# A second Strassen level in three of seven query products, keys and values with held weights, transfers placed anew

## The chip, the core and the metric

The kernel runs on one core of one Trainium2 chip. The metric is device time in microseconds, from launch to the last store: 1040.75 us as the median of three runs (1040.5 to 1040.83). Five queues work beside each other and are synchronised by semaphores: TensorE (PE, whose weight loads the profile shows apart as PEld), VectorE (DVE), ScalarE (ACT), GpSimd (POOL) and SyncE (SP), which here only issues transfers. Each of them works through its instructions in the order in which the program gives them.

## The reference, cut to what matters

Sixty-four batches of 128 tokens with 512 features go through a multi-query attention layer with 16 heads of 64 features; keys and values are shared by the heads.

```python
x = (64, 128, 512);  g_in (512,);  Wq (512, 1024);  Wkv (512, 128);  Wo (1024, 512)
xn  = layernorm(x, g_in)
q   = (xn @ Wq).reshape(b, n, 16, 64).transpose(0, 2, 1, 3) * 64**-0.5
k, v = split(xn @ Wkv)                       # 64 features each
k, v = concat([null_kv[0], k]), concat([null_kv[1], v])
sim = einsum('bhid,bjd->bhij', q, k) + concat([null_bias, attn_bias])
sim = causal and padding mask (sim);  attn = softmax(sim)
out = layernorm(einsum('bhij,bjd->bhid', attn, v).reshape(b, n, 1024) @ Wo, g_out)
return x + out
```

Everything is 32-bit float. The kernel subtracts the null key from every key and the null value from every value, and adds the null value back behind the softmax, so that the null column becomes a constant.

## The kernel before, in words

The batches are worked through in pairs. `cycle(c)` (line 935) writes out by hand one period in which four stages of four different pairs stand side by side: the query product of a pair two cycles ahead, the softmax of the pair (b0, b1), the output projection of the pair before (p, p+1), and the output layernorm of the pair before that (r, r+1). Each cycle ends with `region` (line 914), in which PE does the scores of the next pair and the attention-times-values of the present one in many small matmuls. Cycles run for c = 1 to 29 (line 1226); a prologue fills the pipe and a tail written out by hand empties it. There is no planner: the order of the calls in `cycle` is the order in each queue.

A group is four batches (512 tokens). The **query product** of a group has 4 feature pairs f; for each, `product` (line 480) and `q_one` (line 852) do one level of Strassen's scheme in Winograd's form: the two 256-token halves, the two halves of the 512 input features and the two halves of the 1024 output features are the blocks, and seven products of half size take the place of eight. Product k is two k-steps of a 128x128 weight block against 256 tokens; each such fp32 matmul appears in the trace as two weight loads and two matmuls. The sums that the scheme needs of the tokens are made on POOL (`token_sum`, line 466, four instructions per group, before issued at the end of every odd cycle), those of the weights once at the start. The results are put together from PSUM by ACT copies (`keep`, line 505; `q_out`, line 509) and DVE additions into `qT`. Two of the four feature pairs of a group are done in one cycle (h = 0 and 1), so a group takes an even and an odd cycle. The tile `a` in PSUM is used in turn by products 1, 6, 7 and 4, with a copy by ACT between each two.

**Keys and values** are made by `kv_mm` (line 353): for each batch, the tokens are the held (loaded) operand and the 128 columns of `wkv` stream. `kv_out` (line 369) subtracts the null row. The keys are then turned by DVE in 32x32 blocks and sent through DRAM to become `kT` (`keys_send`, `keys_fetch`, lines 396 and 409, five transfers per group); the values go through DRAM into four copies `vr` (`values_send`, `values_fetch`, five transfers).

The **softmax** of a batch is, per half: scores added on DVE, maximum on DVE, eight exponentials on ACT (`exps`), a reciprocal on DVE (`rinv`), a scaling on POOL (`scale`, line 618), then a block transpose on DVE (`blocks_T`, line 632), after which POOL fills the freed buffer with the bias of a batch two further on (`bias_add`, line 531). The **output projection** (`out_product`, line 743) is Strassen's scheme too; its sums (`out_sum`, line 729) are POOL's.

Of the kernel before, what the change touches and what calls it, by code (L numbers as in the profile page):

```python
# [17 lines left out]
def kernel(  # L18
# [134 lines left out]
    nkv = const.tile([P, KVN], FP, name="nkv")  # L153
# [31 lines left out]
    def load_second():  # L185
        for m in range(XB + 1, 2 * GB):
            load_x(m)
        nc.sync.dma_start(
            out=nkv, in_=cond[0:2].rearrange("r d -> (r d)").partition_broadcast(P)
# [163 lines left out]
    def kv_mm(m, pkv=None):  # L353
        g, t = divmod(m, GB)
        if pkv is None:
            pkv = ps_w.tile([P, KVN], FP, tag="w", name=f"pkv_{m}")
        for kc in range(KC):
            nc.tensor.matmul(  # L358
                pkv,
                xT[g][:, t, kc, :],  # L360
                wkv[:, kc, :],
                start=(kc == 0),
                stop=(kc == KC - 1),
            )
        return pkv

    kvts, kvds = {}, {}

    def kv_out(m, pkv):
        g, t = divmod(m, GB)  # L370
        if t == 0:
            kvts[g] = hp.tile([P, 2, GB, DH], FP, tag="kv", name=f"kvt_{g}", bufs=1)
        nc.vector.tensor_tensor(
            kvts[g][:, :, t, :],
            pkv.rearrange("p (r d) -> p r d", r=2),
            nkv.rearrange("p (r d) -> p r d", r=2),
# [3 lines left out]
    vds, kds = {}, {}  # L380

    def values_send(g):

        vds[g] = dp.tile([P, GB * DH], FP, tag="vd", name=f"vd_{g}")
        nc.sync.dma_start(out=vds[g], in_=kvts[g][:, 1].rearrange("p t d -> p (t d)"))

    def values_fetch(g):
        vr[g] = hp.tile([P, NQ, GB, DH], FP, tag="vr", name=f"vr_{g}")
        src = vds.pop(g).rearrange("(j p) e -> p j e", p=Q)
        for s in range(NQ):  # L390
            nc.sync.dma_start(
                out=vr[g][s * Q : (s + 1) * Q].rearrange("p j t d -> p j (t d)"),
                in_=src,
            )

    def keys_send(g):

        kb = hp.tile([P, 2, GB, Q], FP, tag="kb", name=f"kb_{g}", bufs=1)
        nc.vector.transpose(
            kb,  # L400
            kvts[g][:, 0].rearrange("p t (c k) -> p c t k", k=Q),
        )
        kds[g] = dp.tile([P, 2, GB * Q], FP, tag="kd", name=f"kd_{g}")
        nc.sync.dma_start(
            out=kds[g].rearrange("p c e -> p (c e)"),
            in_=kb.rearrange("p c t q -> p (c t q)"),
        )

    def keys_fetch(g):
        kT[g] = hp.tile([P, NQ, GB, Q], FP, tag="kT", name=f"kT_{g}")  # L410
# [998 lines left out]
```

## Time and profile before

| | |
|---|---|
| runs, median of 3 | 1040.75 us |
| the profiled execution | 1040.6 us; its span 1038.8 us, with 1.8 us around it |
| granted TensorE clock | 0.998 |
| busy, share of the span | PE 99%, PEld 86%, DVE 74%, POOL 68%, ACT 64% |
| idle of POOL until ACT's last attention result, line 741 | 113.0 us in 28 waits |
| one cycle in the middle | 31.45 us |

The times are those of one execution. A matmul's duration in the trace runs over into that of the next, because matmuls are pipelined: what one costs is the distance from its start to the next one's start. In a timeline row the first number is the start in microseconds from the start of the span, the second the stretch that the merged instructions take, "x8" their count, and a bracket tells for how long the engine had been idle and which instruction ended that.

### The profile page before, as it was taken

What the parts mean: (1) busy time and instruction counts of PE and PEld (TensorE: products, weight loads), DVE (VectorE), ACT (ScalarE), POOL (GpSimd) and SP (SyncE); (2) the same over time, 40 slices, a digit from 0 to 9 for tenths busy, and PEclk for the clock granted to TensorE, in tenths of its full rate; (3) what the DMA queues carried; (4) which work ended last, traced back from release to release, by engine and by line L of the source; (5) the groups of instructions that cost most, each with busy time, mean ns of one, the idle gap of its engine ahead of it and who ended that gap; (6) DMA issues with size and microseconds to landing.
All of it is one profiled execution on the core that took longest, in us unless ns stands there. A gap on an engine that the chain in (4) does not pass through costs nothing.

```text
span 1038.8 us, 31012 instructions
## 1 busy us (share of the span) xinstructions
PE 1024.2 (99%) x11856; PEld 896.4 (86%) x11856; DVE 771.2 (74%) x1664; ACT 665.9 (64%) x2799; POOL 711.0 (68%) x530
## 2 busy tenths in 40 slices
PE   8999999999999999999999999999999999999996
PEld 7888888888888888888888888888888888888875
DVE  7776677787677786677776777776786876766688
ACT  2665677565776566776656776657765657765581
POOL 3697767676775857767577676757758587666774
PEclk9999999999999999999999999999999999999999
DMA  6633160432515134151341504334151341502202
GB/s 210 157 121 85 52 182 27 146 92 94 144 52 153 57 120 128 42 169 50 127 112 67 169 25 150 88 103 137 51 154 55 123 125 42 166 12 73 83 11 92
DMA packets 68690, 105.10 MB, mean 101 GB/s; under 512 B 8641, under 2 KB 32833, under 8 KB 66753
## 3 DMA queue, kind: packets, MB, share of 16 engines
q1 hardware_dynamic: 67440, 102.08, 32.3%
q8 instruction: 96, 1.57, 0.7%
q10 hardware_dynamic: 1104, 1.05, 0.3%
q14 instruction: 50, 0.40, 0.1%
HBM read 67.45 MB, written 35.65 MB: 99 GB/s over the span
## 4 chain that ended last, share of the span: by engine, by line
PE 92%; ACT 3%; DVE 3%; DMA 1%; POOL 1%; issue 1%; POOLq 0%; DVEq 0%; ACTq 0%
PE pa L496 20%; PE pyX L758 19%; PE pc L496 10%; PE pyY L758 9%; PE ps L551 9%; PE pkv L358 5%; PE pyw L758 5%; PE pw L496 5%; PE poX L668 4%; PE pq L445 2%; ACT s L599 2%; PE pos L668 2%; PE poY L668 1%; DMA x<-in_x_dram 1%; DVE y_end L821 1%
## 5 line engine op out<-in xcount | busy, mean ns | idle before, releaser
L599 ACT ACTIVATE s<-s,nmax 128x65 f32<-128x65 f32 (+1 forms) x1024 | 377.5, 393 | 0.0
L535 POOL TENSOR_TENSOR s<-biasp,mneg 128x1552 f32<-128x1552 f32 x64 | 206.2, 3223 | 70.6 <-DVE sb L635 58.9
L599 ACT ACTIVATION_READ_ACCUMULATOR s<-s,nmax 128x1 f32 x1024 | 221.3, 216 | 0.0
L620 POOL TENSOR_TENSOR s<-s,rinv 128x1024 f32<-128x1024 f32 (+1 forms) x128 | 190.4, 1488 | 44.5 <-DVE rinv L616 44.5
L635 DVE STREAM_TRANSPOSE sb<-s 128x1536 f32<-128x1536 f32 x64 | 113.5, 1773 | 43.2 <-POOL s L620 43.0
L585 DVE TENSOR_TENSOR s<-ps,s 128x256 f32<-128x256 f32 (+2 forms) x224 | 120.0, 605 | 16.9 <-PE ps L551 14.7
L496 PE MATMUL pa<-xS,wq 128*128 128x256 f32 x480 | 123.4, 379 | 0.5 <-ACT ku L507 0.5
L758 PE MATMUL pyX<-wo,oT 128*128 128x256 f32 x512 | 121.6, 380 | 0.3 <-POOL oT L741 0.3
L741 POOL TENSOR_TENSOR yS<-oT 128x512 f32<-128x512 f32 x32 | 40.9, 1278 | 117.2 <-ACT oT L708 113.0
L708 ACT ACTIVATE oT<-poX,nv 128x256 f32<-128x256 f32 x59 | 28.0, 475 | 143.8 <-PE poX L668 74.4
L590 DVE TENSOR_REDUCE nmax<-s 128x8 f32<-128x520 f32 (+1 forms) x128 | 116.4, 948 | 0.0
L758 PE MATMUL pyX<-wT,oT 128*128 128x256 f32 x488 | 115.4, 379 | 0.3 <-POOL oT L741 0.3
L758 PEld LDWEIGHTS pyX<-wo,oT 128*128 128x128 f32 x512 | 96.8, 190 | 15.3 <-issue 1.3
L758 PEld LDWEIGHTS pyX<-wT,oT 128*128 128x128 f32 x488 | 92.6, 190 | 13.3 <-POOL oT L741 0.7
L496 PEld LDWEIGHTS pa<-xS,wq 128*128 128x128 f32 x480 | 88.9, 190 | 11.7 <-ACT ku L507 0.9
L551 PEld LDWEIGHTS ps<-kT,qT 64*64 64x64 f32 x4096 | 85.6, 134 | 11.5 <-issue 11.4
L551 PE MATMUL ps<-kT,qT 64*64 64x128 f32 (+1 forms) x4096 | 93.7, 245 | 0.6 <-issue 0.6
L517 DVE TENSOR_TENSOR qT<-pc,ku 128x256 f32<-128x256 f32 x120 | 50.4, 420 | 58.6 <-ACT ku L507 43.5
L514 ACT COPY qT<-pa 128x256 f32<-128x256 f32 x60 | 23.0, 383 | 101.7 <-PE pa L496 101.7
L288 POOL TENSOR_TENSOR rstd<-rstd,nhalf 128x1 f32<-128x1 f32 x64 | 35.7, 559 | 66.6 <-DVE rstd L287 66.6
L668 PE MATMUL pos<-sb,vr 32*64 32x128 f32 (+1 forms) x1792 | 81.0, 321 | 0.0
L668 PE MATMUL poY<-sb,vr 32*64 32x128 f32 x720 | 74.4, 347 | 0.0
(113 smaller groups left out, 2299.8 us busy)
## 6 DMA issues: line engine op xcount, KB each, us to landing
x<-in_x_dram SPq DMA_DIRECT2D x64, 256.0 KB, 5.4
res<-in_x_dram SPq DMA_DIRECT2D x64, 256.0 KB, 3.1
out_dram<-y SPq DMA_DIRECT2D x58, 256.0 KB, 2.0
xd<-xb SPq DMA_DIRECT2D x14, 1024.0 KB
xT<-xd SPq DMA_DIRECT2D x56, 256.0 KB, 6.1
vr<-vd SPq DMA_DIRECT2D x64, 128.0 KB, 8.5
kT<-kd SPq DMA_DIRECT2D x64, 64.0 KB, 9.6
kd<-kb SPq DMA_DIRECT2D x16, 128.0 KB
```

Source lines behind the costliest of these rows:

```text
L358: nc.tensor.matmul(pkv, xT[g][:, t, kc, :], wkv[:, kc, :], start=(kc == 0), stop=(kc == KC - 1),)
L496: nc.tensor.matmul(prod[tag], w[:, kc, f * P : (f + 1) * P], t[:, :, kc, :], start=(start and kc == 0), stop=(kc == HK - 1), skip_group_ch ...
L517: nc.vector.tensor_tensor(o, p, k, ALU.add)
L535: nc.gpsimd.tensor_tensor(S[b], biasp, mneg[:, t].unsqueeze(1).broadcast_to([P, R8, ROW]), ALU.add,)
L551: nc.tensor.matmul(to[r][i * DH : (i + 1) * DH, f, :], qT[g][rows, f, t, NQ - 1 - i if hf else i], kT[g][rows, 0 : NQ if hf else NQ // 2, ...
L585: nc.vector.tensor_tensor(sv, ps, sv, ALU.add)
L590: nc.vector.tensor_reduce(nmax[b][:, hf], S[b][:, :, WITH_NULL[hf]], AX.X, ALU.max, negate=True)
L599: nc.scalar.activation(row, row, AF.Exp, bias=nmax[b][:, hf, k : k + 1], accum_out=rsum[b][:, hf, k : k + 1],)
L620: nc.gpsimd.tensor_tensor(sv, sv, rinvs.pop((b, hf)).unsqueeze(2).broadcast_to([P, R8, sv.shape[2]]), ALU.mult,)
L635: nc.vector.transpose(sb.rearrange("p j e q -> p e j q"), S[b][:, :, 1 : ROW - 1].rearrange("p e (j k) -> p e j k", k=Q),)
L668: nc.tensor.matmul(po[s][rows, half], vr[g][quad(s), j, t, :], sb[quad(s), slots, r * NF : (r + 1) * NF, :], start=start, stop=True, skip_ ...
L758: nc.tensor.matmul(prod[key], h[:, c, :], w[:, c, :], start=(start and c == 0), stop=(c == HC - 1), skip_group_check=not start,)
```

## The change

Parts that go together:

- In cycles from c = 2 on (`LEAF = 2`), products 2, 4 and 3 of two feature pairs are taken together (`leaf`). Their 2x2 blocks of 128x128 are multiplied by a second level of the scheme: seven products of 128 output features by 128 input features by 128 tokens in place of eight. They come in four stages that add up in one PSUM tile of three blocks; after each stage DVE adds what is complete onto `qT`.
- What the stages need: sums of tokens on POOL (`leaf_sums`, 12 instructions of 128 columns in every even cycle), sums of weights on POOL once (`leaf_weights`, nine ahead of cycle 1's other work and three at its end), in tiles `wL` and `xL`.
- For c >= 2, products 1, 6 and 7 are copied by ACT straight into `qT` (`first_into`), product 5 is added there by DVE (in `q_one` k = 7 and the new k = 8), and the last copy of the chain (k = 4) goes.
- `qT` becomes four tiles of a quarter group each, in one copy instead of two.
- `kv_mm` holds `wkv` and streams two batches; its result is already the transposed key (partitions 0 to 63) and value (64 to 127). The keys are copied to the other partitions by one transfer; the values are turned by DVE and take two transfers out and one back.
- The calls in `cycle` stand in another order: among others `token_sum` at the top of the even cycle, `load_x`, `store` and the fetches apart from each other, the DVE maxima of b1 ahead of those of b0. The alignment of PE's instructions (`addr_align`) stands at another place with other offsets.

The core of the diff (the prologue's calls follow from it; `q_first`, `stats_part` and `gain_copy` are defined but not called):

```diff
-    def kv_mm(m, pkv=None):
+    def kv_mm(m):
...
+        pkv = ps_w.tile([P, 2 * N], FP, tag="w", name=f"pkv_{m}")
         for kc in range(KC):
             nc.tensor.matmul(
                 pkv,
-                xT[g][:, t, kc, :],
                 wkv[:, kc, :],
+                xT[g][:, t : t + 2, kc, :],
...
+        nc.vector.tensor_scalar(
+            kT[g][:, :, t : t + 2, :],
+            pkv.rearrange("p (t i q) -> p i t q", t=2, q=Q),
+            nkv, None, ALU.subtract,
+        )
...
     def values_send(g):
+        vt = hp.tile([P, NQ, GB, Q], FP, tag="vt", name=f"vt_{g}", bufs=1)
+        nc.vector.transpose(vt[DH:], kT[g][DH:])
...
+    def keys_send(g):
+        nc.sync.dma_start(out=kT[g][DH:], in_=kT[g][:DH])
...
+    def leaf_sums(g, k):
+        n = 4 if k == 3 else 3
+        xL[g, k] = gp.tile([P, n, N], FP, tag=f"xL{k}", name=f"xL{k}_{g}", bufs=1)
...
+        for o, p, m in ((t1, b12, b11), (t3, b22, b12), (t2, b22, t1), (t4, b21, t2)):
+            nc.gpsimd.tensor_tensor(o, p, m, ALU.subtract)
...
+    def leaf(c, k, stage):
...
+            leaves[k] = ps_w.tile([P, 3, N], FP, tag="w", name=f"pl{k}_{g}_{f}")
+        pw, pY, pX = (leaves[k][:, i] for i in range(3))
...
+        def mm(to, w, t, start=False):
+            nc.tensor.matmul(to, w, t, start=start, stop=True, skip_group_check=True)
+        def onto(o, p):
+            nc.vector.tensor_tensor(o, p, o, ALU.add)
...
+        if stage == 0:
+            mm(pX, w11, b11, True)
+            onto(out[:, 0, 0], one(pX))
+        elif stage == 1:
+            mm(pw, w12, b21)
+            mm(pX, v2, t2)
+            mm(pY, v1, t1)
+            onto(out[:, 0], two(leaves[k][:, 0:3:2]))
+            onto(out[:, 1, 1], one(pY))
+        elif stage == 2:
+            mm(pX, w21, t3)
+            mm(pY, v4, b22)
+            onto(out[:, :, 1], two(leaves[k][:, 1:3]))
+        else:
+            mm(pX, w22, t4)
+            onto(out[:, 1, 0], one(pX))
...
         if k == 1:
             product(g, f, 1, ps_q, "a")
-            keep("a", "p1")
+            if c >= LEAF:
+                first_into(g, f, 0)
+            else:
+                keep("a", "p1")
...
+        elif k == 8:
+            o = q_part(g, f, 1)
+            nc.vector.tensor_tensor(o, by_block("c"), o, ALU.add)
```

The order of PE's calls in a cycle from c = 2 on (qk,h is product k of feature pair h; lk.s is stage s of product k's second level): q1,0, l2.0, q5,0, q6,0, out 1, q7,0, out 2, q1,1, l2.1, key_values, q6,1, l2.2, l3.0, out 6, l2.3, q5,1, l3.1, out 5, l4.0, q7,1, out 7, l4.1, out 4, l3.2, l4.2, out 3, l4.3, l3.3, region. POOL's in an even cycle: four token_sum, leaf_sums 2, out_sum 0, pow, leaf_sums 3, out_sum 1, pow, leaf_sums 4, scale(b0,0), pow, out_sum 3, pow, scale(b0,1), out_sum 2, scale(b1,0), scale(b1,1), two bias_add. In ACT's queue the copy of q1,0 stands behind four of the eight `values_out` of the pair.

468 lines of the change are left out of this document (304 added, 164 removed).

## The prediction

> **What bounds the kernel now.** I read the page first (busy times, then the chain of work that ended last), then stretches of single cycles, then PE's timeline inside one.
>
> ```profile
> span 1038.8 us, 31012 instructions
> PE 1024.2 (99%) x11856; PEld 896.4 (86%) x11856; DVE 771.2 (74%) x1664; ACT 665.9 (64%) x2799; POOL 711.0 (68%) x530
> ...
> PE 92%; ACT 3%; DVE 3%; DMA 1%; POOL 1%; issue 1%; POOLq 0%; DVEq 0%; ACTq 0%
> ...
> 473.18:504.63 31.45, 31.45 (x369) 27.69 (x368) 23.09 (x51) 21.01 (x88) 24.28 (x19) 1.00 0.12 44
> 504.63:536.08 31.45, 31.45 (x369) 27.70 (x368) 23.87 (x54) 21.00 (x88) 19.39 (x15) 1.00 0.55 163
> ```
>
> PE holds 92% of the chain. The last two rows are an even and an odd cycle, from one region's start to the next; after the stretch stand the busy times of PE, PEld, DVE, ACT and POOL, then the granted clock. PE is busy in all of both, at full clock, so a cycle is as long as what PE is given to do. DVE has 7.6 to 8.4 us to spare, ACT 10.4, POOL 7.2 (even) and 12.1 (odd). DMA is far from full. So the change is worth what it takes from PE, less what PE must newly wait for.
>
> **What PE's work costs.** The price of a matmul is the distance from its start to the next start:
>
> ```profile
> 464.39 1.03 PE L496 MATMUL pa<-xS,wS 128*128 128x256 f32 x4
> 465.26 1.05 PE L358 MATMUL pkv<-wkv,xT 128*128 128x128 f32 x8
> 466.15 1.03 PE L496 MATMUL pa<-xS,wq 128*128 128x256 f32 x4
> 467.01 1.05 PE L358 MATMUL pkv<-wkv,xT 128*128 128x128 f32 x8
> 467.90 1.89 PE L758 MATMUL pyY<-wo,oT 128*128 128x256 f32 x8
> 469.63 1.03 PE L496 MATMUL pc<-xT,wS 128*128 128x256 f32 x4
> ...
> 465.04 1.08 PEld L358 LDWEIGHTS pkv<-wkv,xT 128*128 128x128 f32 x8
> ```
>
> Eight matmuls of 256 columns take 469.63 - 467.90 = 1.73 us; eight of 128 take 0.89 us (466.15 - 465.26, and again 467.90 - 467.01), hardly more than half, although each has its own weight load. The group behind is not late either.
>
> Second level: a product of two feature pairs was 8 matmul instructions of 256 columns (2 pairs x 2 k-steps x 2 instructions), 1.73 us. It becomes 7 blocks x 2 = 14 of 128 columns, 14/8 x 0.89 = 1.56 us. Three products a cycle, cycles 2 to 29: 3 x 28 x 0.17 = **14.5 us less** (0.1725 before rounding). Keys and values: 16 of 128 columns per pair of batches (1.78 us) become 8 of 256 (1.73 us): 0.05 x 32 pairs = **1.6 us less**. PE alone would bring 1040.6 to 1024.5.
>
> [...]
>
> **What the other queues get.**
>
> ```profile
> L517 DVE TENSOR_TENSOR qT<-pc,ku 128x256 f32<-128x256 f32 x120 | 50.4, 420 | 58.6 <-ACT ku L507 43.5 <-PE pc L496 13.2
> L373 DVE TENSOR_TENSOR kvt<-pkv,nkv 128x128 f32<-128x128 f32 x64 | 18.0, 282 | 3.5 <-PE pkv L358 3.4
> L399 DVE STREAM_TRANSPOSE kb<-kvt 128x256 f32<-128x256 f32 x16 | 6.5, 408 | 0.0
> L330 DVE STREAM_TRANSPOSE xb<-x 128x512 f32<-128x512 f32 x56 | 35.9, 680 | 0.0
> L514 ACT COPY qT<-pa 128x256 f32<-128x256 f32 x60 | 23.0, 383 | 101.7 <-PE pa L496 101.7
> ```
>
> DVE, per cycle: 6 additions at 0.42, 2 key-value subtractions at 0.28 and half a 0.41 transpose go (3.3 us). There come 4 additions for products 5 (1.7), per second-level product 3 of 128 columns and 2 of 256 (0.84 + 0.84, three times 5.1), one subtraction at 0.42, half a transpose at 0.68. That is 7.5, net +4.2 us: 23.1 to 23.9 becomes about 27.3 to 28.1 of a 30.9 us cycle. It fits, with some 3 us left for waiting. ACT loses two copies (0.77 us).
>
> In-order waits are the danger: a stage adds into a PSUM block that DVE must have read after the stage before. Between the stages of one product PE has 1.7 to 6.2 us of other work (out 3 alone between l4.2 and l4.3; out 4 and l3.2, 2.2 us, between l4.1 and l4.2). The tightest is the latter: DVE takes l4.1 only behind `blocks_T(b1)` and the projection's addition. Laying the new order out with the old durations, DVE is done with it about when PE comes to l4.2. I take nothing for it; the upper side is in the range.
>
> A wait that I do count is before q6,0, which overwrites `a` once ACT has copied q1,0 out:
>
> ```profile
> 478.47 1.13 PE L496 MATMUL pa<-xT,wq 128*128 128x256 f32 x4
> 479.44 1.03 PE L496 MATMUL pw<-xT,wq 128*128 128x256 f32 x4
> 480.31 1.03 PE L496 MATMUL pc<-xS,wS 128*128 128x256 f32 x4
> ...
> 478.62 0.47 ACT L708 ACTIVATE oT<-poX,nv 128x256 f32<-128x256 f32 x1 [4.96 <-PE pos L668]
> ...
> 480.06 0.39 ACT L507 COPY kp<-pa 128x256 f32<-128x256 f32 x1
> ...
> 968.92 0.36 ACT L507 COPY ku<-pa 128x256 f32<-128x256 f32 x1
> ...
> 969.33 1.13 PE L496 MATMUL pa<-xS,wq 128*128 128x256 f32 x4 [0.51 <-ACT ku L507]
> 970.30 1.89 PE L758 MATMUL pyY<-wo,oT 128*128 128x256 f32 x8
> ```
>
> Before, products 2 and 5 stand between them; now l2.0 (2 instructions, 0.22) and product 5 (0.87). q6,0 would start at 479.44 + 0.22 + 0.87 = 480.53. ACT's copy stands behind four `values_out` as before and ends at 480.45. The last rows show what such a release costs: copy end 969.28, start 969.33, and the four matmuls take 0.97 instead of 0.86. So 480.45 + 0.05 + 0.11 = 480.61, 0.08 us late: 28 x 0.08 = **2.2 us more**. What is queued behind it on PE is out 1, for which nobody is in a hurry.
>
> POOL gets 12 instructions of 128 columns in each of 14 even cycles, a width that it does not have now:
>
> ```profile
> L478 POOL TENSOR_TENSOR xS<-xT 128x512 f32<-128x512 f32 x30 | 38.4, 1280 | 0.0
> L727 POOL TENSOR_TENSOR wT<-wo 128x1024 f32<-128x1024 f32 x1 | 2.4, 2371 | 0.0
> L802 POOL TENSOR_TENSOR rstdo<-rstdo,nhalf 128x1 f32<-128x1 f32 x64 | 36.6, 574 | 21.8 <-DVE rstdo L798 21.8
> masks.py:199 POOL TENSOR_SCALAR_AFFINE_SELECT ident<-ident 128x128 f32<-128x128 f32 x1 | 0.3, 294 | 0.1
> ...
> 479.27 1.27 POOL L478 TENSOR_TENSOR xS<-xT,xS 128x512 f32<-128x512 f32 x1
> 482.00 1.27 POOL L741 TENSOR_TENSOR yS<-oT 128x512 f32<-128x512 f32 x1 [1.45 <-ACT oT L708]
> ...
> 489.43 1.92 POOL L620 TENSOR_TENSOR s<-s,rinv 128x1024 f32<-128x1024 f32 x1
> ...
> 73.62 1.47 POOL L741 TENSOR_TENSOR yS<-oT 128x512 f32<-128x512 f32 x1
> 75.17 1.27 POOL L741 TENSOR_TENSOR oT<-yS,oT 128x512 f32<-128x512 f32 x1
> ```
>
> From below the price is 0.29 us (affine select, one input), from above 1.28 (four times the columns). The line through 512 and 1024 columns gives 0.46 at 128 and 0.73 at 256; I take it, as the same operation. The first four, 1.8 us, fall into the idle 1.45 us behind the token sums. The other eight delay `scale(b0,1)`: from 482.00, 3.5 us into the cycle, POOL has two out_sum, two pow, scale, pow, out_sum, pow, scale = 8.7 us by the starts of the old rows, and 8 x 0.46 = 3.7, so it ends 15.9 us into the cycle. By my layout DVE comes to `blocks_T(b0)` at the same point. I take nothing for it. Once, ahead of cycle 1, come nine weight sums, 9 x 0.73 = 6.6 us, at a place where POOL does not idle (73.62 follows the output weights' sums without a gap), so cycles 1 and 2 are late by what their slack doesn't hold. Between 0 and 8.8 us (all twelve) I take **2 us more**.
>
> Transfers and SP: ten for keys and values in two cycles become four; none was on the path.
>
> ```profile
> vr<-vd SPq DMA_DIRECT2D x64, 128.0 KB, 8.5
> kT<-kd SPq DMA_DIRECT2D x64, 64.0 KB, 9.6
> ```
>
> They are needed a cycle after they are sent. `values_send` and `keys_send` now wait on SP for DVE's turning at the even cycle's end; behind them stand the residual loads and the next x load, which are used 7 us or more later. I cost this at nothing. If that cover went, an x load would delay `norm_stats` on DVE.
>
> The sum: 1040.6 - 14.5 - 1.6 + 2.2 + 2 = 1028.7. That is against the profiled execution (span 1038.8, 1.8 around it); the median is 0.15 above it, so **1029 us**.
>
> **Instruction supply.** PE's stalls without a releaser ("issue") are another unknown:
>
> ```profile
> PEld ps L551 <- issue: 11.4, 33, 0.7
> PEld pa L496 <- issue: 11.2, 29, 0.4
> ```
>
> There is one at the region's start and one behind it in each cycle; on PE each costs about 0.1 us (478.47: 0.97 to the next start instead of 0.86). PE gets 378 matmul instructions per cycle in place of 368, and the alignment moves. Both pauses gone would give 28 x 0.2 = 5.6 us more gain, one more as long as PEld's (0.35) would cost 9.8. I take no change.
>
> **The rivals.** First: the new waits are more than I count. For it: DVE at nine tenths, in order, with about twelve more points per cycle at which PE waits for it. Against it: most of them have 2 us of other work between. At 0.3 us more per cycle, 28 x 0.3 = 8.4: **1037 us**. Chance 0.17.
>
> Second, slower than before: POOL. Place: the eight `leaf_sums` ahead of the scalings of b0. The layout holds up to 0.46 us each; from there a further 0.1 makes each even cycle 0.8 us late, since `blocks_T(b0)` holds DVE, which holds l3.1 and all behind it: 14 x 0.8 = 11 us. It eats the whole gain of 11.9 us from 0.57 on, which is the price of the 128x1 power in the rows above. At 0.64, half the 512-column price, 0.18 x 8 x 14 = 20 us: **1049 us**. For it: a fixed cost per POOL instruction, as that power shows. Against it: affine select at 0.29. Chance 0.10.
>
> Third: the weight loads bind. In the key-value run the eight loads start (1.08 - 0.19)/7 = 0.127 us apart while the matmuls start 0.111 apart, so the loads lose their lead. At 0.127, 14 cost 1.78 us, 0.05 more than 8 wide ones: 84 x 0.05 = 4.2 more, 1.6 less, 4.2 of waits: **1047 us**. Against it: the longest run of narrow ones now is eight (l3.2 with l4.2), the same length as the run that shows no loss. [...] Chance 0.05.
>
> **How the numbers follow.** The forecast, 1024 to 1034, has 0.66; the rivals 0.17, 0.10 and 0.05; 0.02 is for something else. A difference under 0.2% (2 us) can't be told from no change. Faster: the forecast and four fifths of the first rival, 0.80; same 0.05; slower 0.15. The range goes from 1022 (PE's full gain and half of the pauses) to 1043 (the first rival and POOL at its break-even), which leaves out the worse part of the second rival and the third.
>
> **What would show it.** Right: a cycle of about 31.0 us, matmuls of the second level 0.111 us apart, DVE busy 27 to 28 us of it, a wait of PE on ACT at q6,0. POOL's 128-column row near 0.46. Wrong: PE idle before stages of `leaf` released by DVE (first rival), POOL's row over 0.55 with `blocks_T` waiting for `scale` (second), narrow matmuls 0.12 apart or more (third).

## The result, and the profile after

The changed kernel takes **1166.8 us** (median of 4 runs, 1161.6 to 1171.3) against 1040.8 for the kernel before on the same chip: 1.121 times as long, 95% interval 1.116 to 1.126. The forecast was 1029. The profiled execution spans 1167.0 us, 2.1 less than its own time.

In the rows, `x` are the token loads (`load_x`), `xd` the turned tokens on their way out to DRAM (`tokens_out`), `xT` the same tokens fetched back (`tokens_in`), `res` the residual rows (`load_res`) and `m` the mask; `pl` is the PSUM tile of a second-level product, `pkv` that of keys and values, `pos` one of attention times values. First the page, then one even and one odd cycle, from region to region (columns as in the prediction), then the waits: engine and tile, what it waited for, us in all, times, the longest.

```profile
span 1167.0 us, 31412 instructions
PE 1055.9 (90%) x12104; PEld 914.4 (78%) x12104; DVE 902.6 (77%) x1996; ACT 645.7 (55%) x2743; POOL 787.8 (68%) x710
```

```profile
464.52:495.76 31.24, 31.24 (x379) 27.77 (x378) 26.49 (x63) 20.20 (x86) 27.60 (x29) 1.00 0.07 27
495.76:536.72 40.96, 33.79 (x379) 28.84 (x379) 30.14 (x66) 20.30 (x86) 19.40 (x15) 0.96 0.47 131
```

```profile
DVE st L283 <- DMA x<-in_x_dram: 69.6, 19, 6.1
...
PE pl L554 <- DVE qT L557: 40.9, 21, 2.6
...
PE pkv L357 <- DMA xT<-xd: 33.7, 12, 5.0
```

The even cycle is 0.2 us shorter than before, as a gain of the second level should look, and PE fills it. The odd one is 9.5 longer, and PE stands idle in 7 us of it. Over cycles 6 to 27 the means are 31.5 and 31.5 before, 31.3 and 40.8 after. So the loss is made in odd cycles, in which tokens are fetched and a mask is made. The three waits are new (before, DVE waited 0.8 us for x in all), and this is one odd cycle: what SP issues, then where PE and DVE stop, with the idle time in brackets.

```profile
497.04 1.30 SPq L386 DMA_DIRECT2D vd<-vt  x2
498.43 1.34 SPq L392 DMA_DIRECT2D kT<-kT  x1
499.82 1.07 SPq L137 DMA_DIRECT2D res<-in_x_dram  x2
500.93 0.59 SPq L127 DMA_DIRECT2D x<-in_x_dram  x1
501.69 2.69 SPq L347 DMA_DIRECT2D xT<-xd  x4
504.48 0.59 SPq L127 DMA_DIRECT2D x<-in_x_dram  x1
505.12 0.47 SPq L144 DMA_DIRECT2D m<-in_mask_BxS_bk_dram  x1
505.69 0.54 SPq L396 DMA_DIRECT2D vr<-vd  x1
```

```profile
500.73 0.32 PE L771 MATMUL pos<-sb,vr 32*64 32x128 f32 x1 [1.64 <-issue]
...
515.17 2.83 PE L357 MATMUL pkv<-xT,wkv 128*128 128x256 f32 x8 [3.00 <-DMA xT<-xd]
517.80 1.89 PE L598 MATMUL pa<-xS,wS 128*128 128x256 f32 x4
519.51 0.43 PE L554 MATMUL pl<-xL,wq 128*128 128x128 f32 x2
...
524.65 0.49 PE L554 MATMUL pl<-xT,wq 128*128 128x128 f32 x2 [2.53 <-DVE qT L557]
```

```profile
517.66 0.69 DVE L283 BATCH_NORM_STATS2 st<-x 128x6 f32<-128x512 f32 x1 [5.42 <-DMA x<-in_x_dram]
...
519.66 3.15 DVE L626 TENSOR_SCALAR mneg<-m 128x256 f32<-128x256 uint8 x2
```

PE stops three times: in the region without a releaser, for the tokens, and for a leaf's addition. DVE had stood 5.4 us for x and then spent 3.15 us on the mask.

The stops make up 7.2 of the 9.5 us. Most of the rest is in the clock, 0.96 in the row of this cycle: in the trace it stands at 0.50 from 516.1 to 519.5 us, right behind the 3.00 us stop, and the four matmuls from 517.80 on take 1.71 us in place of 0.86. There are twelve such stretches of 3.4 or 6.8 us in the cycles, 44 us in all, and none before. At full clock their work would have taken half as long, so they cost some 22 us, an estimate from their length and PE's busy time in them. From region 0 to region 29 the changed kernel takes 127.5 us more; PE is idle for 97.1 of that (before, 0.6), and the half clock has the 22. The other 8, and the some 16 that PE's smaller work should have given, are in delays that no row names.

The trace's DMA completions for these issues, in us, and for the same transfers of before:

```
after                    issued   landed
x (m), one transfer      500.93   507.7 to 510.4, in 4 parts
xT, four transfers       501.69   last parts 511.8, 512.6, 514.3, 515.0
x (m+1)                  504.48   514.7 to 517.6, in 4 parts
vr                       505.69   519.9 to 524.5, in 4 parts
before
x (m)                    507.22   515.8 to 516.0, in 4 parts   used by DVE 523.25
xT                       519.84   last part 527.5              used by PE 528.16
```

A token load has an outer dimension of four and lands in four parts, which I read as four DMA engines, an estimate: from 514 to 518 us, with x and vr under way, 26.1% of 16 engines are busy, which is 4.2 (the DMA view of this stretch: packets, MB, share of 16 engines):

```profile
q1 hardware_dynamic: 174, 0.39, 26.1%
```

The listing also shows what had been near: before, xT came some 0.7 us ahead of its use. Its fetch and its use in the trace of before, and the mask there:

```profile
519.84 1.80 SPq L347 DMA_DIRECT2D xT<-xd  x4
```

```profile
528.16 1.05 PE L358 MATMUL pkv<-wkv,xT 128*128 128x128 f32 x8
```

```profile
511.80 0.62 DVE L525 TENSOR_SCALAR mneg<-m 128x256 f32<-128x256 uint8 x2
```

The change brings the uses forward: keys and values are wanted 16.4 us after the region's start (515.17 - 3.00 - 495.76) and not 23.5 (528.16 - 504.63). The fetch is issued sooner too, 5.9 us after that start and not 15.2 (501.69 - 495.76, 519.84 - 504.63), but behind the residual rows and a token load it takes 13.3 us to land, not 7.7. So xT lands 3.6 us sooner for a use that comes 7.1 us sooner.

### The profile page after: what moved, and what is told of

Its sections match the earlier page's. It is cut to its first block, busy times and chain, and to the rows that moved or that the text cites. A ratio compares the mean times of both kernels' runs of the same rounds, so it can differ in the third digit from the quotient of the medians.

```text
span 1167.0 us, 31412 instructions
## 1 busy us (share of the span) xinstructions
PE 1055.9 (90%) x12104; PEld 914.4 (78%) x12104; DVE 902.6 (77%) x1996; ACT 645.7 (55%) x2743; POOL 787.8 (68%) x710
## 3 DMA queue, kind: packets, MB, share of 16 engines
q8 instruction: 96, 1.57, 0.6%
## 5 line engine op out<-in xcount | busy, mean ns | idle before, releaser
L702 ACT ACTIVATION_READ_ACCUMULATOR s<-s,nmax 128x1 f32 x1024 | 232.0, 227 | 0.0
L557 DVE TENSOR_TENSOR qT<-pl,qT 128x128 f32<-128x128 f32 (+1 forms) x420 | 127.0, 330 | 28.9 <-PE pl L554 28.1
L861 PE MATMUL pyX<-wT,oT 128*128 128x256 f32 x488 | 118.3, 385 | 0.3 <-POOL oT L844 0.3
L771 PE MATMUL pos<-sb,vr 32*64 32x128 f32 (+1 forms) x1792 | 87.8, 323 | 18.8 <-issue 18.7
L357 PE MATMUL pkv<-xT,wkv 128*128 128x256 f32 x256 | 70.4, 424 | 33.8 <-DMA xT<-xd 33.7
L283 DVE BATCH_NORM_STATS2 st<-x 128x6 f32<-128x512 f32 x64 | 44.0, 687 | 69.6 <-DMA x<-in_x_dram 69.6
L861 PEld LDWEIGHTS pyX<-wT,oT 128*128 128x128 f32 x488 | 88.2, 190 | 11.4 <-POOL oT L844 0.7
L933 ACT ACTIVATE yn<-y,nmro,rstdo 128x512 f32<-128x512 f32 x56 | 45.2, 807 | 92.3 <-DVE nmro L925 92.3
L288 POOL TENSOR_TENSOR rstd<-rstd,nhalf 128x1 f32<-128x1 f32 x64 | 35.7, 559 | 87.5 <-DVE rstd L287 84.8
L357 PEld LDWEIGHTS pkv<-xT,wkv 128*128 128x128 f32 x256 | 51.6, 211 | 43.1 <-issue 34.7
```

Of the source, the lines that this page charges most:

```text
L357: nc.tensor.matmul(pkv, wkv[:, kc, :], xT[g][:, t : t + 2, kc, :], start=(kc == 0), stop=(kc == KC - 1),)
L557: nc.vector.tensor_tensor(o, p, o, ALU.add)
L702: nc.scalar.activation(row, row, AF.Exp, bias=nmax[b][:, hf, k : k + 1], accum_out=rsum[b][:, hf, k : k + 1],)
L771: nc.tensor.matmul(po[s][rows, half], vr[g][quad(s), j, t, :], sb[quad(s), slots, r * NF : (r + 1) * NF, :], start=start, stop=True, skip_ ...
L861: nc.tensor.matmul(prod[key], h[:, c, :], w[:, c, :], start=(start and c == 0), stop=(c == HC - 1), skip_group_check=not start,)
L933: nc.scalar.activation(yn[b], ys[b], AF.Identity, bias=nmr, scale=rstd)
```

## The experiments

Theory A: late token loads and tokens. Rival B: the second level's own waits on DVE. C: something else in odd cycles. Behind each time stand its ratio to the kernel before and the 95% interval of that ratio. e1 to e4 ask which of these it is.

**e1**, both token loads ahead of the tokens.

```
         if m < B:
             load_x(m)
+        if m + 1 < B:
+            load_x(m + 1)
...
-        if m + 1 < B:
-            load_x(m + 1)
```

> Edit: in every cycle the second token load x(m+1) is issued right behind the first, ahead of the four xT fetches. Theory A (backlog): a token load is finished by four of the sixteen DMA engines alone (its completions come late on four), so on these four the x loads, a share of xT and the value fetch stand in one line; putting a second x load ahead of xT moves the wait, it does not remove it: xT lands some 5 us later, PE's wait before the key-value product in odd cycles grows from about 3 us to about 8, the wait of DVE on x goes; sum 1170 to 1195 us. Rival B (only x(m+1) is late, and DVE's blocked queue is the cost): that wait goes and the time falls by 40 us or more, to about 1125. Rival C (VectorE has too much to do with the second level): no change, about 1167.

1175.0 us, 1.129 [1.126, 1.132]. The wait moved: DVE for x 20.1 us in all, PE for xT 76.2, PE for leaf additions 3.4.

**e2**, the tokens first, then both loads.

```
             values_out(p, (0, 2))
+        if not first and (m - 2) // GB < NG:
+            tokens_in((m - 2) // GB)
         if m < B:
             load_x(m)
+        if m + 1 < B:
+            load_x(m + 1)
...
-        if not first and (m - 2) // GB < NG:
-            tokens_in((m - 2) // GB)
...
-        if m + 1 < B:
-            load_x(m + 1)
```

> Edit: in every cycle the four xT fetches are issued first, then both token loads. Theory A (backlog on four DMA engines): the wait of PE for xT goes (13 odd cycles of 3 us), the second token load lands where it did, at 16 us into the odd cycle, so DVE is still late and PE waits before the second level's stages instead; the time falls by 10 to 35 us, to 1130 to 1157. Rival B (only x(m+1) is late): about 1167, since x(m+1) is as late as before. Rival C (VectorE's load): about 1130 with the waits on DVE as they were.

1149.1 us, 1.104 [1.098, 1.110]. PE's wait for xT is gone; DVE waits 44.4 for x; PE waits 33.5 for leaf additions and 22.7 for a late DVE ahead of the key-value product. Whatever stands behind in the queue is late: A.

**e3**, each token load as four transfers of 32 rows.

```
-            nc.sync.dma_start(out=xs[m], in_=x[g * GB : (g + 1) * GB, t * Q : (t + 1) * Q, :])
+            for j in range(GB):
+                nc.sync.dma_start(
+                    out=xs[m][j * Q : (j + 1) * Q], in_=x[g * GB + j, t * Q : (t + 1) * Q, :])
```

> Edit: each token load is issued as four transfers of 32 rows, one per batch, instead of one with the four batches as its outer dimension; same bytes, same place. Theory A: each of the four then ends on all sixteen DMA engines, xT is no longer held up on four of them and x(m+1) lands within 12 us of the cycle's start; the waits for xT (about 43 us in all) and most of the waits of the second level on DVE (about 42 us) go: 1085 to 1105 us. Rival C (VectorE's load): the waits on DVE stay, about 1125 to 1135. What neither touches: the pauses in the region (21 us).

1115.4 us, 1.072 [1.066, 1.077]: 51 us back, less than A said. The same bytes now land in 16 parts, and PE no longer waits for xT. But the waits for leaf additions stayed, 32.5 us. From the waits of e3:

```profile
DVE st L284 <- DMA x<-in_x_dram: 13.0, 11, 3.8
...
PE pl L555 <- DVE qT L558: 32.5, 15, 2.6
...
PE pos L772 <- issue: 18.6, 12, 1.8
```

**e4**, the changed kernel's order with one-level products: each `c >= LEAF` and `c < LEAF` in `q_one` and `cycle` that chooses between leaf and product reads 99, and the calls of `leaf_weights` and `leaf_sums` are gone.

```
-        if c >= LEAF:
+        if c >= 99:
             leaf(c, 2, 0)
```

> Edit: the changed kernel's transfers, key-value product and order of calls, but products 2, 4 and 3 in one level in every cycle, with no leaf sums. Theory A (transfers): odd cycles stay long, PE's wait for xT stays at about 3 us each, DVE still waits for x; total 1095 to 1150 us. Rival C (the second level loads VectorE and POOL): the odd cycles become as short as the even ones, about 1040 to 1055 us.

1124.9 us, 1.081 [1.073, 1.089]. Without a second level most of the loss stays, so B alone is not the cause. How much of it is B's this run cannot tell: it has other waits in its place, 17.3 and 18.2 us for ACT's copies of the query product and of the output. Even cycles are longer (32.8), odd ones shorter (35.7); PE, with more to do, waits only 9.4 us for xT.

In e3 DVE is late in odd cycles without waiting for anything. From the timeline of e3, DVE's row for the mask and POOL's rows at that time:

```profile
495.54 2.77 DVE L627 TENSOR_SCALAR mneg<-m 128x256 f32<-128x256 uint8 x2
```

```profile
494.84 1.92 POOL L724 TENSOR_TENSOR s<-s,rinv 128x1024 f32<-128x1024 f32 x1
496.70 1.33 POOL L845 TENSOR_TENSOR oT<-oT,oT 128x512 f32<-128x512 f32 x1
```

**e5**: e3 with the mask moved to the top of the cycle, where POOL is idle.

```
         if fin:
             pair_stats(r + 1)
+        if c % 2 and n0 < B:
+            mask_neg(n0 // GB)
...
         key_values(b0 + 6)
-        if c % 2 and n0 < B:
-            mask_neg(n0 // GB)
```

> The kernel of e3_x_by_batch (token loads as four transfers of 32 rows) with one more edit: in odd cycles mask_neg stands right behind pair_stats(r+1), where POOL has nothing to do, and no longer behind kv_out, where POOL's scale and out_sum run. In e3_x_by_batch the two mask instructions took 2.77 us together at 495.54 us beside POOL's work, and TensorE then waited 2.5 us in each odd cycle for an add of a leaf (qT) on DVE. Theory A (the mask is held up by POOL and passes that on to the leaf's adds): the two mask instructions take some 0.9 us, the waits of pl on DVE qT (27.6 us over 11 odd cycles) fall under 5, time 1075 to 1090 us. Rival (DVE is late there for the sum of its work, wherever the mask stands): the waits stay above 20 and the time is 1108 to 1118.

1069.2 us, 1.027 [1.025, 1.029], 46 us under e3. DVE's row for the mask in e5, then the waits of e5:

```profile
466.46 0.62 DVE L627 TENSOR_SCALAR mneg<-m 128x256 f32<-128x256 uint8 x2
```

```profile
PE pos L772 <- issue: 19.3, 13, 1.8
...
PE pkv L358 <- DMA xT<-xd: 1.8, 1, 1.8
...
PE pl L555 <- DVE qT L558: 1.1, 3, 0.5
```

0.62 us in place of 2.77, as before the change, and the waits for leaf additions are gone, with the second level in place: that settles B. In e3 the two mask instructions end at 496.90 and 498.31 us, 0.14 and 0.28 behind the two of POOL above, which end at 496.76 and 498.03; in the changed kernel they end at 521.41 and 522.81, 0.15 and 0.28 behind POOL's at 521.26 and 522.53. So I read that each is held up until POOL's is over; by what, no run shows. Not all of the 46 us is the mask's own time: the stretches of half clock fell from nine to one, worth some 13 us by the estimate above. Of the three stops of PE only the pause without a releaser is left.

**e6**: e5 with the sends of values and keys behind `key_values`. **e7**: the changed kernel with the mask of e5 and these sends, its token loads whole again.

```
         key_values(b0 + 6)
+        if first and send < NG:
+            values_send(send)
+            keys_send(send)
...
         if first and toks:
             tokens_out(m // GB)
...
-        if first and send < NG:
-            values_send(send)
-            keys_send(send)
```

> e5_mask_earlier and one more edit: in even cycles values_send and keys_send stand right behind key_values, some 12 us before the region, and no longer right ahead of it, so that their small packets are over when the region runs. TensorE pauses once for 1.8 us at the start of the values' matmuls of each even cycle's end (pos, released by nothing that the profile shows; weight loads pause as well), 19 to 21 us in all. Theory A (the instructions that TensorE needs next come late because of those packets): the pauses fall under 5 us in all, time 16 to 22 us under e5_mask_earlier, some 1060 to 1070. Rival B (the pause belongs to the place of the code in memory alone, as the alignment sets it): it stays at 1.8 us, time within 5 us of e5_mask_earlier. Rival C: values_fetch or the stores are now late and give a new wait.

> The changed kernel with only the two edits of e5 and e6 (mask earlier, send earlier); the token loads are one transfer each again, as in the changed kernel. Theory A (three separate causes: late token loads and tokens, the mask behind POOL, the pause): the pauses go, the token waits stay (pkv on xT and st on x some 5 us together in each odd cycle), and the mask's part goes only as far as the wait on x does not make DVE late in its place: 1115 to 1140 us. Rival (the mask or the pause alone makes the others): under 1090.

1092.5 us, 1.050 [1.047, 1.052], and 1093.6 us, 1.051 [1.049, 1.052]. Both missed. The pause grew to 2.9 us (33.2 and 32.3 in all), so taking the small packets away does not cure it. What grew it is probably that SP, no longer held at its wait for DVE's turned values, now issues the residual rows 1.1 us ahead of the region and a token load 0.4 us into it (3.9 and 5.0 us into it in e5), right behind xd; no run tests that alone. For the same reason e7 hardly waits for x (8.4) or xT with whole loads: they are issued sooner. In these runs the form of a load matters only where it is issued late.

What feeds the pause is in the DMA view. It has a queue of the kind instruction, q8, with 96 packets of 16 KB in a run (1.57 MB in the changed kernel's). I read it as TensorE's, an estimate from the counts: 24208 loads and matmuls and 331 NOPs of that kernel are 95.9 blocks of 256 instructions, the unit of the alignment in the code. e5's DMA view in two stretches, 455 to 458.6 and 458.6 to 459.4 us (packets, MB, share of the engines), then PE's timeline; the region starts at 456.1:

```profile
q1 hardware_dynamic: 152, 1.05, 72.3%
issues: line engine op xcount, KB each, median us to landing
vd<-vt SPq DMA_DIRECT2D x2, 64.0 KB, 3.2
...
q1 hardware_dynamic: 597, 0.07, 57.6%
q8 instruction: 1, 0.02, 7.3%
```

```profile
456.07 2.91 PE L653 MATMUL ps<-kT,qT 64*64 64x128 f32 x128
...
459.11 0.27 PE L772 MATMUL pos<-sb,vr 32*64 32x128 f32 x1
460.96 0.32 PE L772 MATMUL pos<-sb,vr 32*64 32x128 f32 x1 [1.58 <-issue]
```

First the 1 MB of `tokens_out` (xd), then the packet. Its starts in the middle cycles, counted from the region's start, against xd's issue:

```
                           xd issued   packet starts   pause
e5, end of even cycles     -1.44       2.5 to 2.7      1.5 to 1.8
e5, end of odd cycles      none        0.2 to 0.8      none
e6, end of even cycles     -1.44       3.4 to 3.7      2.5 to 2.9
before, even               2.1         -1.6 to -1.0    none
```

The alignment's offset 223 leaves 33 instructions to the end of a block: 4 of the last leaf stage and 29 of the scores. 256 further on are 14 pairs of load and matmul of the values, and there PE stops. So I read from these starts that a packet is asked for as one block ends (29 instructions of the scores are 0.3 us) and needed at the end of the next, which here is the 3 us of the scores.

**e8**: e5 with `tokens_out` behind the sends, as before the change. **e9**: e8 with whole loads. **e10**: the changed kernel with this edit alone.

```
-        if first and toks:
-            tokens_out(m // GB)
...
             keys_send(send)
+        if first and toks:
+            tokens_out(m // GB)
```

> e5_mask_earlier with one edit: at the end of even cycles tokens_out stands behind values_send and keys_send, as it did in the kernel before, so that its transfer starts some 3 us into the region and no longer 1.4 us ahead of it. Theory A (TensorE's instructions come in packets of 16 KB on a queue of their own; the packet for the values' matmuls starts 0.3 us into the region where nothing is under way, but 2.5 to 2.7 us into it behind the 8 KB packets of tokens_out, and is then late): the packet starts at 0.3 to 0.5 us, the pause of 1.6 us goes, and the time is 1069 - 13 x 1.6 = 1048 (1044 to 1053). Rival B (the small packets of the two sends delay it): the pause stays, 1065 to 1071. Rival C: the tokens, sent some 4 us later, come late for kv; a wait of pkv on xT.

> e8_tokens_out_after_send with the token loads as one transfer each again (so the changed kernel with the mask moved up and tokens_out behind the sends). Theory A (a load with an outer dimension of four lands on four DMA engines and comes late when it is issued among others): waits of DVE on x and of TensorE on xT return, 3 to 6 us in each odd cycle, 1080 to 1110 us. Rival (once the mask and the pause are gone there is time enough for them): within 5 us of e8.

> The changed kernel with tokens_out behind the two sends as its only edit. Theory A (separate causes): the pause goes (21 us), the waits on x and xT and those of pl on DVE stay or grow, since the tokens come later: 1140 to 1165 us. Rival (the pause makes the others): under 1120.

e8: 1106.8 us, 1.063 [1.060, 1.067]; e9: 1147.95, 1.103 [1.101, 1.105]; e10: 1183.7, 1.137 [1.135, 1.139]. All three are slower than forecast. The pause is gone and the packet starts 0.4 to 1.1 us into the region at most even ends, much as A said, but rival C came true: xd goes out 3.25 us into the region, and the later tokens cost more than the pause had. PE waits for xT (the row names the last of several DMAs) 36 us in e8, 73 in e9 and 74 in e10. The waits of e8:

```profile
PE pkv L358 <- DMA m<-in_mask_BxS_bk_dram: 33.1, 10, 3.6
...
PE pkv L358 <- DMA xT<-xd: 2.7, 1, 2.7
```

**e11**: e5 with the code's alignment moved, and no transfer.

```
+        if soft and first and c >= 4:
+            nc.tensor.addr_align(256, offset=250)
         out_one(p, 3)
...
-        if soft:
+        if soft and not (first and c >= 4):
             nc.tensor.addr_align(256, offset=...)
```

> e5_mask_earlier with tokens_out where it was; in even cycles from 4 on the alignment of TensorE's code stands ahead of the last product of the output and so that a block of 256 instructions ends some 1.6 us ahead of the region, not 0.3 us into it. No transfer is moved. Theory A (a block's packet is asked for when the block before the last ends, and must come within the 256 instructions between, which here are the scores, 3 us): the packet starts ahead of tokens_out's packets, the pause goes or falls under 0.5 us, 1045 to 1055 us. Rival B (the pause goes with the transfers at that time, wherever the blocks end): it stays at 1.6 us, 1065 to 1072.

1339.3 us, 1.288 [1.286, 1.291]. The edit missed its aim: moved in even cycles only, the alignment needs more filling in every cycle, and filling is executed. It stands in the trace as NOPs, 215 and 54 in turn where e5 has 6 and 7, and PE waits up to 15 us a time for it (`pl`, issue, 194.9 us in all). The time says nothing about the pause.

**e12**: e8 with the tokens ahead of the token loads, and the residual rows of even cycles' ends behind both. **e13**: e8 with odd cycles' token loads issued in the even cycle before. **e14**: e13 with whole loads. **e15**: e13 without the second level (the edit of e4).

```
+        if not first and (m - 2) // GB < NG:
+            tokens_in((m - 2) // GB)
         if m < B:
             load_x(m)
...
             load_x(m + 1)
+        if fin and r not in res:
+            load_res(r)
+            load_res(r + 1)
...
-        if pair:
+        if pair and (not first or not toks):
             load_res(p)
```

That was e12; e13:

```
-        if m < B:
+        if m < B and (first or c == 1):
             load_x(m)
...
-        if m + 1 < B:
+        if m + 1 < B and (first or c == 1):
             load_x(m + 1)
...
             store(r + 1)
+        if first and m + 3 < B:
+            load_x(m + 2)
+            load_x(m + 3)
```

> e8_tokens_out_after_send (1106.8 us, pause gone, TensorE waits 3.5 us per odd cycle for xT, which lands 17 to 18 us after the start of the region) with a new order on SP in odd cycles: the fetch of the tokens first, then the two token loads, then the two residual rows that even cycles sent ahead of their region. 768 KB less stand ahead of the tokens; 256 KB of tokens or x took about 1.3 us there. Theory A (bytes ahead of xT in one queue): xT lands 3 to 4 us earlier, the wait goes, and with no pause and no wait an odd cycle is 31.2 to 31.6 us like the even ones: 1038 to 1048 us in all. Rival (the two token loads take the place of the tokens: norm_stats of DVE waits for x and hands it to the leaf's adds): 1055 to 1080. Nothing in A leads below 1036: even cycles of 31.2 against 31.45 give 3.7 us, and the first six cycles are together some 5 us longer than before.

> e8_tokens_out_after_send with one edit: the two token loads of odd cycles (512 KB) are issued in the even cycle before, behind its stores, some 6 us ahead of the region, where the DMA engines stood nearly idle (share 0.08 in even cycles of e5_mask_earlier against 0.5 in odd ones); in odd cycles only the residual rows stand ahead of the tokens. Three dates have to be met in an odd cycle: x by 12.7 us and xT by 17.5 us from the start of the region, and nothing large on the engines at 0.3 us, when TensorE's next packet of instructions starts. Theory A (each loss was one missed date, and the three do not hang together otherwise): x lands ahead of the region, xT at 13 to 15 us, the pause stays away: no wait of TensorE over 0.3 us in odd cycles, cycles of 31.2 and 31.3 to 31.7, 1039 to 1049 us. Rival (the loads ahead of the region now delay the packet): the pause is back, 1060 to 1075.

> e13_x_loads_in_even_cycles with the token loads as one transfer each, as in the changed kernel. Theory A: a whole load lands on four engines and takes longer, some 5 to 7 us, but has a whole cycle; it only reaches into the region's first microseconds and can then meet the packet of instructions or the two sends: within 6 us of e13, rather above it. Rival (the whole load delays tokens_out on its four engines and with it xT): 1060 or more.

> e13_x_loads_in_even_cycles with products 2, 4 and 3 of one level, without the leaf's sums: what the second level is worth where no transfer is late. TensorE has 0.52 us more of matmuls in each of 28 cycles, 14.5 us. In e4_no_second_level the one-level products also waited 0.8 us per cycle for ScalarE's copy at q1 of the second pair, which belongs to the order and not to the products: some 22 us more. Theory A (the second level does save what the matmuls' spacing says): 14.5 + 22 = 36 us above e13, at least 12 above. Rival (POOL and DVE, which carry the second level's sums, cost as much as TensorE saves): within 5 us of e13 or under it.

e12: 1138.9 us, 1.094 [1.092, 1.096]; DVE waits 68.7 for x, and hands it on to PE: the rival. e13: 1094.35, 1.051 [1.049, 1.054], far from the 1039 to 1049 expected; e14: 1096.05, 1.051 [1.047, 1.054]. In these two x is early, but xT, fetched only once xd has landed, 9 to 10 us after the region's start, still comes at 17.6 for a use at about 15: PE waits 28.4 and 31.5. With its loads early, the whole form costs nothing measurable. e15: 1097.15, 1.053 [1.050, 1.056], level with e13. Its odd cycles are 33.9 against e13's 35.2, its even ones 32.9 against 31.3: with more work for PE, the wait for xT is only 6.8 us. But its even cycles are not a price of the second level, as the one-level products also wait for ACT's copy in this order of calls:

```profile
PE pa L599 <- ACT qT L616: 17.1, 30, 1.0
```

So e15 shows only that, with xT late, the kernel with a second level waits for what its PE saves. What the second level is worth by itself, with every transfer on time, no run shows; the second level in the old order of calls was not tried either.

**e16**: e5 with the alignment moved alike in all cycles. **e17**: e16 with the residual rows behind the token loads (the last two of e12's edits). **e18**: e17 with a shift of 40 instructions, not 51.

```
+        if soft:
+            nc.tensor.addr_align(256, offset={1: 215, 2: 229, 3: 243, B // 2 - 3: 236}.get(c, 254))
         out_one(p, 3)
...
-        if soft:
-            nc.tensor.addr_align(256, offset={1: 184, 2: 198, 3: 212, B // 2 - 3: 205}.get(c, 223))
```

> e5_mask_earlier with the alignment of TensorE's code moved in every cycle alike, from behind the last leaf to ahead of the last product of the output and by 51 instructions, so that a block of 256 ends some 2 us ahead of the region. In e11_code_earlier only even cycles were moved, so that the filling between one alignment and the next grew to most of a block in every cycle, which cost 5 us in even and 14 us in odd cycles and hid what was asked; moved alike, the filling grows by 51 instructions once. No transfer is moved: tokens_out's packets still start 1.4 us ahead of the region. Theory A (a block's packet is asked for when the block two ahead of it ends, and a large transfer in that moment makes it late): the packet starts before 0.5 us ahead of the region's start, the pause of the values' matmuls (2.2 us with what stands behind it) goes, odd cycles of 31.2 to 31.8 us in place of 33.4, 1037 to 1047 us. Rival (the pause goes with tokens_out's transfer wherever the blocks end): it stays, 1066 to 1072.

> e16_code_earlier_all_cycles with one edit: the two residual rows (512 KB) that even cycles sent ahead of their region go behind the token loads of the odd cycle, so that the tokens are asked for some 2.6 us earlier. In e16 the pause is gone, but TensorE, 2.2 us sooner there, waits 1.5 us per odd cycle for xT in its place. Theory A (bytes ahead of xT in one queue, nothing else left): that wait goes, odd cycles of 31.2 to 31.8 us, 1064.6 - 13 x 1.5 = 1045 (1041 to 1050). Rival (in e12 the same edit, with the loads also behind the tokens, made x late): waits of DVE on x and new ones, 1055 to 1075. It cannot come under 1040: even cycles save 0.25 us each, 3.8 us in all, and the first cycles are some 8 us longer than before, 4 of them the filling.

> e17_tokens_ahead_of_residual with the alignment moved by 40 instructions in place of 51: the block then ends 11 instructions nearer to the region, some 1 us ahead of it. Theory A: the packet still starts ahead of tokens_out's packets or among the first of them, the pause stays away, and the filling costs some 1 us less: 0 to 2 us under e17. Rival: the packet is behind tokens_out again and the pause is back in odd cycles, 15 to 30 us above e17.

e16: 1064.6 us, 1.023 [1.021, 1.024]. xd still goes out 1.44 us ahead of the region, but the packet starts 1.2 to 1.8 us ahead of it in the middle cycles (the DMA view from 454.0 to 455.2 us, region at 455.9, holds it alone), and no pause is left. With e8, in which xd alone was moved, that settles the pause's cause: a packet that starts behind xd. The time missed its forecast all the same and fell by 5 us only, as PE, sooner there, waits for xT. That DMA view, and the waits of e16:

```profile
q8 instruction: 1, 0.02, 5.5%
issues: line engine op xcount, KB each, median us to landing
xd<-xb SPq DMA_DIRECT2D x1, 1024.0 KB, 4.2
```

```profile
PE pkv L358 <- DMA m<-in_mask_BxS_bk_dram: 8.7, 6, 2.0
...
PE pkv L358 <- DMA xT<-xd: 4.8, 4, 1.9
```

e17: 1052.2 us, 1.011 [1.010, 1.013]; 512 KB less ahead of the tokens took 12 us away. e18: 1049.0 us, 1.008 [1.007, 1.009]; PE still waits 4 us in all there for the tokens. A neighbouring odd, even and odd cycle of e18:

```profile
385.60:417.70 32.10, 31.52 (x382) 27.69 (x382) 27.41 (x67) 20.28 (x86) 19.54 (x15) 1.00 0.60 166
417.70:448.90 31.20, 31.20 (x380) 27.70 (x380) 26.46 (x64) 20.20 (x86) 29.17 (x31) 1.00 0.07 27
448.90:480.90 32.00, 31.50 (x383) 27.74 (x382) 27.46 (x67) 20.31 (x86) 19.61 (x15) 1.00 0.60 168
```

All that was changed in it is places of transfers, of one DVE operation and of code; 118 of the 126 us are back. No version beat the kernel before. The sends of e6 together with the alignment of e16 were not tried.

## Why the prediction was wrong

**The step that failed** is "Transfers and SP: ten for keys and values in two cycles become four; none was on the path. They are needed a cycle after they are sent. [...] I cost this at nothing." It weighed the transfers that were removed and only named those that were moved. For the next x load it had 7 us or more from issue to use, and did not hold that against the time to land, 8.8 us in the cycle of before listed above and 9.5 and some 13 after. e3 alone gives 51 us, and e8 to e17 show the tokens again and again. The rows that would have told were in the trace of before, the 0.7 us between xT's landing and its use: the change moved that use 7.1 us forward and the landing only 3.6. The text had the right sign for a lost cover, "an x load would delay `norm_stats` on DVE"; the price of it was missing, and the tokens.

**The mask** was in no step. Moved behind the keys and values it met POOL's scaling and sum: 46 us between e3 and e5, with the clock that came back, the second large term. The diff shows the move, and directly ahead of the new place `scale(b0, 1)` and `out_sum(p, 2)`.

**The clock** was in no step either: the sums are at full clock throughout, as the trace of before was, and the stretches of half clock behind PE's stops added some 22 us.

**Instruction supply**, "I take no change": it was a term of some 20 us in the changed kernel (18.7 by PE's waits for `pos`), and some 2.0 us per odd cycle in e5 counting what stands behind the pause (4.4 to 4.6 us of values in most of them against 2.45 in even cycles). What it hung on was not the pauses of before but a large transfer in front of the packet.

**Second level, 14.5 us, and keys and values, 1.6**: for PE's own work the mechanism was right. Leaf matmuls start 0.111 us apart, 42 in 4.67 us where 24 took 5.18, 0.51 per cycle as forecast, and keys and values 1.73. Yet even cycles gained only 0.25 of these 0.56 us; some 0.2 are lost at q5,0 and q6,0, whose four matmuls take 0.99 and 0.94 us in place of 0.86, where the prediction had 0.08. The odd cycles of e18 are still 0.5 longer than before, and cycles 1 to 6 are 6.5 longer in all (the 2 us of weight sums, late tokens and the filling are in that and were not separated). That is where the rest of the gain went.

**POOL** was right to the hundredth: 128 columns cost 0.459 us, forecast 0.46, and nothing waited for it in the way of the second rival.

```profile
L535 POOL TENSOR_TENSOR xL<-xT 128x128 f32<-128x128 f32 x56 | 24.5, 459 | 0.0
```

**DVE's load**, forecast 27 to 28 us a cycle, is 26.5 and 27.4, and it fits, as e18 shows with 0.7 us of waits for leaf additions in all. The sign named for the first rival, PE idle at leaf stages for DVE, did come, 40.9 us, but by the mask and the late x and not by DVE's load. The third rival is out at 0.111 us.

## What to carry to other kernels

Where a change moves transfers, write down for each its landing and its use in the trace of before, and the use after the change: a transfer off the path by 0.7 us is on it once its reader moves 7 us forward and its landing only 3.6. When the busy engine gets faster, everything that it reads must come earlier, so look at the bytes ahead of the first late transfer in its queue before anything else. And a cure for one wait is only measured when the next date is met as well: of eighteen versions, several removed the wait that they aimed at and were slower for it (e8, e10).

## What the runs showed of the hardware that was not expected

- TensorE's instructions come as 96 packets of 16 KB in a run (q8, by the counts above), which the DMA view counts on the same 16 engines as the data. With 1 MB issued 1.4 us ahead of a stretch of 256 instructions that lasts 3 us, the next packet started 2.5 to 2.7 us into the stretch; where nothing stood in front, mostly 0.3 to 0.5. At 11 ns an instruction (2.91 us for 128 loads and 128 matmuls) PE was soon through the stretch and then stood for 1.5 to 1.8 us. That cost 2.0 us a time (e5 against e16).
- The filling of an alignment is executed: 51 more NOPs (382 in e16's trace, 331 in e5's) made cycle 1 about 4 us longer (37.4 us in e16, 33.5 in e5), and 215 in a row take 15.9 us in e11.
- A stop of PE cost more than its length: behind one of 3.00 us the granted clock was at 0.50 for 3.4 us. e5, whose stops last at most 1.8 us, has one such stretch; the twelve of the changed kernel come with stops of 2.2 to 5.0 us, and its stop of 3.92 us from 657.5 us on has none behind it. Which stop brings one was not tested.
- The two mask instructions of DVE, 0.62 us together, took 2.77 and 3.15 us beside POOL's scaling and sum, and this shows as longer instructions, not as a wait.
